# A four-layer graph network with experts: incidence blocks built in steps inside the attention's tile loop

## The chip, the cores and the metric

The kernel is one program on one core of one Trainium2 chip. The metric is the device time of a whole execution in microseconds (us); of several executions the median is taken. Besides, one execution is recorded by the hardware profiler, and all views of the profile are of that one execution. Engines are named as in the profile: PE is TensorE (PEld its weight loads), DVE is VectorE, ACT is ScalarE, POOL is GpSimd, SP is SyncE. [...]in this kernel the order within each queue is fixed when the program is built.

## The reference, cut to what matters

The network has 3125 nodes with 256 features each, and 53125 edges sorted by destination (25000 random edges, the same edges turned round, and one loop per node). Four layers of a graph operation and a mixture of experts follow each other:

```python
x = x + attention(layernorm(x), edge_attr_8, ..., src, dst)   # layer 0, graph
x = x + experts0(layernorm(x), ...)                           # layer 0, experts
x = x + conv1(layernorm(x), ..., edge_index)                  # three hidden convolutions
x = x + experts1(layernorm(x), ...)
x = x + conv2(layernorm(x), edge_index, ...)
x = x + experts2(layernorm(x), ...)
x = x + conv3(layernorm(x), ..., src, dst)
x = x + slices(layernorm(x), ...)
```

Only layer 0 and the preparation of the convolutions matter here:

```python
def attention(nfeat, attn_bias, Wq, Wk, Wv, Wo, src, dst):
    q, k, v = (heads of nfeat @ Wq.T / SCALING, nfeat @ Wk.T, nfeat @ Wv.T)   # 8 heads of 32
    attn = einsum('ehd,ehd->eh', k[src], q[dst]) + attn_bias
    a = exp(attn - segment_max(attn, dst)[dst])
    a = a / segment_sum(a, dst)[dst]
    return segment_sum(v[src] * a, dst) @ Wo.T

def conv(h, ...):            # in each convolution, with weights of its own
    agg = segment_sum(h[src], dst)      # scaled by degrees of destinations or sources
```

The convolutions need sums over edges, `segment_sum(h[src], dst)`. The kernel computes them as dense matrix products: a 3125 x 3125 matrix of counts, whose entry for a pair of nodes is the number of edges between them, times h. That matrix of counts, in two layouts, is what this document calls **the blocks**.

## The kernel before, in words

**Attention.** `attention()` first prepares: `edges_in()` gathers the edges' sources, destinations and biases in windows of 128 edges per partition row and turns them with TensorE, so that an edge lies on a partition (`src_i`, `row_h`, `eb`); beside it layer norm and the projections q, k, v of all nodes are computed, and k and v are stored in DRAM as one table `kv_d` with a row of 512 values per node. Then follows a loop over T = 25 tiles of P = 125 destination nodes. The edges of one tile fill up to WC = 18 chunks of 128 edges, worked in three parts of PC = 6 chunks. For a tile the functions are called in this order, two tiles being under way at a time:

- `one_hot` (L1551): DVE compares, for all edges of the tile, their destination row with 0..124; the result `oh` has 128 x 2250 elements. `one_hot_turned`: PE turns it, ACT copies the result.
- `logits`, once per part: GpSimd issues six gathers (L1574), each of 128 rows of `kv_d` by the index of the source, into a part of a `kv` buffer (seven of them in rotation); PE brings q to the edges (L1582 into `qx`), DVE multiplies k by it (L1585) and sums per head.
- `sums_of` (L1601 with the bias `eb`, an exponential on ACT, 18 small matmuls into `sm`): sums over the edges of a node; `weights_of`: the weights (L1611, L1613).
- `weighted`: DVE multiplies v by the weights (L1621), ACT makes a float copy `oh_f` of the one-hot matrix, PE sums the weighted v in `acc` (L1628). With its last matmul the `kv` buffers are free for gathers of a later tile.
- `normed`, `normed_turned`, `projected`: division by the sums, the product with Wo, and the addition to x.

The scheduler that builds the program may move instructions of the loop against one another on an engine within the limits of the buffers.

**Blocks and first experts.** After the attention `blocks()` and `experts0()` run interleaved: `blocks` is a generator, and `experts0` advances it at nine points in each of its seven groups of three or four tiles. `blocks` divides the nodes of a tile into GT = 25 groups of GN = 5 destinations, G = 625 groups in all, of at most 128 edges each (otherwise a flag sends the run to a general path). From the degrees, which the attention has counted in `deg`, it computes the first edge of each group, stores these 625 numbers in DRAM, gathers the edges of each group by them (L1750), and derives for every edge the row and tile of its source and its column in the group. Then for each of 25 tiles: `hot` compares (L1790: `hr`, `hc` of 128 x 3125 elements, `hs` of 128 x 625), PE counts, with one matmul per group into a "bk" bank of 125 columns (L1802), and degrees of sources into `bdeg` (L1804), seven evacuations take the counts to `ab`, alternately on DVE and ACT (`evacuate`, L173 and L175), `ab` is written to `at_d` in DRAM (L1808), PE turns `ab` piece by piece (L1814), four evacuations take it to `an`, which is written to `an_d` (L1818). Three rows of scales (`to_row`, L1693 to L1699) are written to `rows_d`.

`experts0` loads its weights in `wslot`, and for each group of tiles computes layer norm, gates, hidden layers and the sum, which is added to x (L776); the gates' chain (softmax, choice of two, turning) is short instructions in a row.

The convolutions that follow read `at_d` and `an_d` back.

Of the kernel before, what the change touches and what calls it, by code (L numbers as in the profile page):

```python
# [56 lines left out]
def gnn_ffn_kernel(ctx: ExitStack, tc: tile.TileContext, a, out: bass.AP):  # L57
# [1353 lines left out]
    def attention():  # L1411
# [5 lines left out]
        q_d = dram.tile([P, T, 3, D], BF16, name="q_d")  # L1417
        win_d = dram.tile([T * WC], I32, name="win_d")
        KO, VO, AO = 16, 16 + D, 7
        WB = T * WC // 5  # L1420
        with ExitStack() as es:
            big = es.enter_context(tc.tile_pool(name="att", bufs=1))
            wqkv = big.tile([128, 2, 3 * D], F32, name="wqkv")
# [3 lines left out]
            eb = big.tile([128, H, T * WC], F32, name="eb")  # L1427
# [4 lines left out]


            setup = ExitStack()
            pool = setup.enter_context(tc.tile_pool(name="att_in", bufs=2))
            psum = setup.enter_context(tc.tile_pool(name="ps_in", bufs=2, space=PSUM))
# [50 lines left out]
            def turned(to, b, w):  # L1487
                ps = psum.tile([128, 512], F32, name="tr")
                nc.tensor.transpose(ps[:, :WB], w, ident[:WB, :WB])
                evacuate(to[:, b * WB:(b + 1) * WB], ps[:, :WB])  # L1490

            def edges_in():
# [5 lines left out]
                for name, to in (("src", src_f), ("dst", dst_f)):  # L1498
                    for b, w in windows(a[name].rearrange("(e o) -> e o", o=1), 1, "w_" + name):
                        wf = pool.tile([WB, 128], F32, name="wf")  # L1500
                        nc.vector.tensor_copy(wf, w)
                        turned(to, b, wf)
# [3 lines left out]
                yield  # L1506
                for b, w in windows(a["edge_attr_8"], H, "w_eb"):
                    for h in range(H):
                        turned(eb[:, h, :], b, w.rearrange("p (e h) -> p e h", h=H)[:, :, h])
                    yield  # L1510
# [4 lines left out]
            for i, (t0, n) in enumerate(GROUPS):  # L1515
# [6 lines left out]
                for i_ in range(n):  # L1522
                    p1 = psum.tile([P, 512], F32, name="p1")
                    p2 = psum.tile([P, D], F32, name="p2")
# [17 lines left out]
            psum = es.enter_context(tc.tile_pool(name="ps_att", bufs=3, space=PSUM))  # L1542
# [4 lines left out]
            def one_hot(t):  # L1547
# [7 lines left out]
                nc.sync.dma_start(s.q, q_d[:, t])  # L1555
                return s
# [11 lines left out]
            def logits(s, p):  # L1568

                kv = pool.tile([128, PC, 2 * D + KO], F32, name="kv", bufs=7)  # L1570
# [19 lines left out]
            def sums_of(s):  # L1590
                c = slice(s.t * WC, (s.t + 1) * WC)

                nc.vector.scalar_tensor_tensor(s.l, s.l, 640.0, eb[:, :, c].rearrange("p h c -> p c h"),
# [24 lines left out]
            def weighted(s):  # L1618
                s.acc = psum.tile([P, 512], F32, name="acc", bufs=2)
# [33 lines left out]

            now, before = one_hot(0), None
            one_hot_turned(now)
            for t in range(T + 1):
                if now:
                    logits(now, 0)
                if before:
                    weights_of(before)  # L1660
                    weighted(before)
                after = one_hot(t + 1) if t + 1 < T else None
                if before:
                    normed(before)
                if after:
                    one_hot_turned(after)
                if now:
                    logits(now, 1)
                if before:
                    normed_turned(before)  # L1670
                if now:
                    logits(now, 2)
                if before:
                    projected(before)
                if now:
                    sums_of(now)
                before, now = now, after

# [12 lines left out]
            nc.vector.tensor_reduce(flags[:, 3:4], fan(ok), AX.X, ALU.add)  # L1691

# [8 lines left out]
    def blocks(pool, psum):  # L1701

        ptr_d = dram.tile([G], I32, name="ptr_d")
        iota_h = pool.tile([128, P], BF16, name="iota_h", bufs=1)
        nc.vector.tensor_copy(iota_h, iota[:, :P])

        upto = pool.tile([P, GT], F32, name="upto", bufs=1)
        within = pool.tile([P, GT], F32, name="within", bufs=1)
        gn = pool.tile([P, GT + 1], F32, name="gn", bufs=1)
        nc.vector.tensor_scalar(gn, iota[:P, :GT + 1], float(GN), None, ALU.mult)  # L1710
        nc.vector.tensor_scalar(upto, gn[:, :GT], pcol[:P], None, ALU.is_gt)
        nc.vector.tensor_scalar(within, gn[:, 1:], pcol[:P], None, ALU.is_gt)
        nc.vector.tensor_sub(within, within, upto)
        ps = psum.tile([128, 512], F32, name="bk")
        for i, l in enumerate((upto, ones[:P, :GT], within)):
            nc.tensor.matmul(ps[:GT, i * 128:i * 128 + T], l, deg, start=True, stop=True)
        got = pool.tile([GT, 3, T], F32, name="got", bufs=1)
        nc.vector.tensor_copy(got, ps[:GT, :384].rearrange("p (a t) -> p a t", a=3)[:, :, :T])
        first = pool.tile([GT, T], F32, name="first", bufs=1)
        nil = pool.tile([GT, T], F32, name="nil", bufs=1)  # L1720
        nc.vector.memset(nil, 0.0)
        nc.vector.tensor_tensor_scan(first, got[:, 1, :], nil, 0.0, ALU.add, ALU.add)
        nc.vector.tensor_sub(first, first, got[:, 1, :])
        nc.vector.tensor_add(first, first, got[:, 0, :])
        ptr = pool.tile([GT, T], I32, name="ptr", bufs=1)
        nc.vector.tensor_scalar(ptr, first, float(E - 128), None, ALU.min)
        nc.sync.dma_start(ptr_d.rearrange("(t g) -> g t", g=GT), ptr)

        over = pool.tile([GT, T], F32, name="over", bufs=1)
        nc.vector.tensor_scalar(over, got[:, 2, :], 128.5, None, ALU.is_gt)  # L1730
# [399 lines left out]
```

## Time and profile before

| | |
|---|---|
| timed executions | 4295.15, 4304.97, 4306.31 us; median 4304.97 |
| profiled execution | 4563.24 us; its span 4561.5 us; mean granted clock of TensorE 0.867 |
| busy in the span | PE 83%, PEld 55%, DVE 37%, ACT 19%, POOL 14% |
| preparation of the attention, 0 to 239 us | PE 125.44, DVE 104.34, ACT 41.05, POOL 59.27 us busy; clock 0.78 |
| tile loop of the attention, 239 to 1118 us | shown in the prediction |
| blocks beside the first experts, 1118 to 1671 us | shown in the prediction |
| everything after, 1671 to 4561 us | PE 2672.24, DVE 709.09, ACT 527.92, POOL 120.86 us busy; clock 0.95 |

The page of the profile has the busy time of each engine, the granted clock in 40 slices, the DMA queues, the chain of work that ended last, and the costliest groups of instructions. A group is a line of the code with an engine and an operation: its busy time, the mean duration of one instruction in nanoseconds, and the idle time of its engine just before these instructions, with what released the engine most often. Busy time by stage is a view of its own, as are the waits of a stretch, the timeline of an engine and the chain in order of time. A share over the whole span mixes stages with different limits; the stages are therefore read one by one.

The ends of the experts' seven groups (the last addition at L776 of each) are at 1233.7, 1366.7, 1476.2, 1562.5, 1607.1, 1640.6 and 1671.3 us; the last addition of the attention is at 1118.3 us.

### The profile page before, as it was taken

Reading aid. Unit: us, or ns where it says so; the run is one execution under the profiler, and the core shown is the slowest. Engines: PE = TensorE matmul, PEld = TensorE weight load, DVE = VectorE, ACT = ScalarE, POOL = GpSimd, SP = SyncE. Lnnn points to the kernel's source line nnn. Section 1 sums busy time; section 2 is a strip of 40 time slices with the busy share of each in tenths; the row PEclk is TensorE's granted clock in tenths of the full one; section 3 lists DMA queues with packets and bytes.
Section 4 is the critical chain, followed back from the end, with each engine's and each line's share of the span. In section 5 each row is a group of like instructions: output and inputs, shape, how many; then the busy total and the mean of one; then the engine's idle time right before and its main releaser. Section 6 shows DMA issues by size and latency. Waiting matters only on the chain.

```text
span 4561.5 us, 47103 instructions
## 1 busy us (share of the span) xinstructions
PE 3807.8 (83%) x19103; PEld 2519.1 (55%) x19103; DVE 1675.1 (37%) x3696; ACT 848.6 (19%) x1496; POOL 623.3 (14%) x585
## 2 busy tenths in 40 slices
PE   5466666666688889999999799991998999999996
PEld 3255555555566454555656578881455555554564
DVE  5255555556887550111124611113314111140271
ACT  1111111112223230101101122220202332320030
POOL 1345555452100000000001300005000000000000
PEclk9677777777676689999999899996997999999997
DMA  3444444443232613222222155552320000012100
GB/s 111 151 124 132 132 131 130 130 131 88 77 119 104 235 71 103 75 92 73 83 73 77 51 177 183 185 182 75 106 71 15 14 7 14 12 53 95 54 1 29
DMA packets 283806, 429.65 MB, mean 94 GB/s; under 512 B 32565, under 2 KB 231817, under 8 KB 283578
## 3 DMA queue, kind: packets, MB, share of 16 engines
q1 hardware_dynamic: 189524, 248.19, 16.4%
q0 software_dynamic: 50480, 133.87, 10.2%
q10 hardware_dynamic: 43573, 44.48, 3.0%
q8 instruction: 152, 2.49, 0.2%
q14 instruction: 77, 0.62, 0.0%
HBM read 330.75 MB, written 95.61 MB: 93 GB/s over the span
## 4 chain that ended last, share of the span: by engine, by line
PE 60%; DMA 2%; DVE 2%; ACT 1%; issue 1%; POOL 0%; ACTq 0%; SPq 0%; DVEq 0%; POOLq 0%
PE agg L1865 22%; PE po L207 17%; PE hid_ps L207 12%; PE tr L207 2%; PE row L207 1%; DMA y<-ys_d,row 1%; PE tok L1324 1%; PE po L205 1%; PE tr L197 1%; PE tr L1946 1%; DMA blk<-at_d 0%; POOL y L1079 0%; ACT h L1171 0%; PE s L207 0%; PE tr L1059 0%
## 5 line engine op out<-in xcount | busy, mean ns | idle before, releaser
L1865 PE MATMUL agg<-blk,hp 125*128 125x500 bf16 (+1 forms) x5250 | 1015.0, 354 | 104.2 <-DMA blk<-at_d 97.6
L1865 PEld LDWEIGHTS <-hp 125*128 125x128 bf16 x5250 | 509.7, 97 | 591.7 <-ACT hp L1836 90.7
L1574 POOL DMA_INDIRECT kv<-kv_d,src_w x450 | 472.6, 1050 | 482.1 <-PE acc L1628 285.7
L1887 DVE TENSOR_TENSOR at<-agg,scale_row 128x500 f32<-128x500 f32 (+1 forms) x70 | 41.9, 623 | 858.6 <-PE agg L1865 684.8
L1582 PE MATMUL qx<-q_t,oht 125*128 125x256 bf16 x1350 | 255.7, 366 | 62.1 <-issue 26.6
L1177 DVE SCALAR_TENSOR_TENSOR x<-po,gall,x 125x256 f32<-125x256 f32 x200 | 94.0, 484 | 426.1 <-PE po L207 426.1
L947 POOL DMA_INDIRECT xs_d<-r_l,pos x50 | 59.6, 1193 | 1391.2 <-ACT r_lt L175 1245.6
L207 PE MATMUL hid_ps<-xe,wslot 128*128 128x256 f32 x1024 | 242.3, 389 | 7.7 <-DVE xe L1061 7.3
L1582 PEld LDWEIGHTS <-oht 125*128 125x128 bf16 x1350 | 169.9, 129 | 124.3 <-issue 47.9
L1171 ACT ACTIVATE h<-hid_ps,shift,scale 128x500 f32<-128x500 f32 (+1 forms) x224 | 161.7, 723 | 375.6 <-PE hid_ps L207 366.7
L1628 PE MATMUL acc<-kv,oh_f 128*125 128x265 f32 x900 | 226.8, 415 | 3.4 <-DVE kv L1621 3.4
L207 PE MATMUL po<-wslot,hid 128*128 128x256 f32 x1024 | 226.2, 379 | 0.0
L207 PEld LDWEIGHTS hid_ps<-xe,wslot 128*128 128x128 f32 x1024 | 182.0, 191 | 52.2 <-DVE xe L1061 16.5
L207 PEld LDWEIGHTS po<-wslot,hid 128*128 128x128 f32 x1024 | 194.6, 190 | 26.5
L1628 PEld LDWEIGHTS acc<-kv,oh_f 128*125 128x125 f32 x900 | 183.6, 207 | 42.7 <-DVE kv L1621 4.0
L207 PE MATMUL po<-wslot,h 128*125 128x256 f32 x800 | 203.8, 389 | 0.1
L207 PE MATMUL hid_ps<-h,wslot 128*128 128x500 f32 (+1 forms) x448 | 192.8, 551 | 4.1 <-ACT h L1171 0.5
L1585 DVE TENSOR_TENSOR kv<-kv,qx 128x512 f32<-128x512 f32 x225 | 151.0, 681 | 110.5 <-remote 63.4
L207 PE MATMUL hid_ps<-xt,wslot 128*128 128x500 f32 (+1 forms) x448 | 189.0, 545 | 0.0
L207 PEld LDWEIGHTS po<-wslot,h 128*125 128x125 f32 x800 | 146.6, 189 | 73.0 <-ACT h L1171 25.3
L1068 ACT ACTIVATE hid<-hid_ps,wslot 128x256 f32<-128x256 f32 x256 | 118.5, 474 | 342.7 <-PE hid_ps L207 342.7
L1611 PE MATMUL sm<-m,oht 125*128 125x8 bf16 x450 | 15.6, 168 | 187.7 <-DVE kv L1577 186.6
(449 smaller groups left out, 4839.0 us busy)
## 6 DMA issues: line engine op xcount, KB each, us to landing
wslot<-in_ex_W SPq DMA_DIRECT2D x64, 1024.0 KB
blk<-an_d SPq DMA_DIRECT2D x60, 610.4 KB
xs_d<-nothing ACTq DMA_DIRECT2D x8, 3328.0 KB
blk<-at_d SPq DMA_DIRECT2D x40, 610.4 KB
blk<-an_d SPq DMA_DIRECT2D x45, 457.8 KB
at_d<-ab SPq DMA_DIRECT2D x25, 762.9 KB
an_d<-an SPq DMA_DIRECT2D x25, 762.9 KB
blk<-at_d SPq DMA_DIRECT2D x30, 457.8 KB
```

What stands on the lines that cost most here:

```text
L197: nc.tensor.transpose(ps[:, i * P:(i + 1) * P], src[:, i, k * 128:(k + 1) * 128], ident[:P, :P])
L205: nc.tensor.matmul(ps, ones_h[:, :ps.shape[0]], bias, start=True, stop=False)
L207: nc.tensor.matmul(ps, l, r, start=(bias is None and i == 0), stop=(i == last))
L947: st = nc.gpsimd.indirect_dma_start(out=xs_d, in_=l2[:, i, :], in_offset=None, out_offset=bass.IndirectOffsetOnAxis(ap=self.pos[s][:, t0 + ...
L1068: nc.scalar.activation(hid[:, m, :], ps[:, :BLK], AF.Gelu, bias=c[:, 4 + m:5 + m])
L1171: nc.scalar.activation(dst[:, m, :c], ps[:, :c], AF.Relu, bias=shift[:, l, col:col + 1], scale=scale[:, l, col:col + 1])
L1177: nc.vector.scalar_tensor_tensor(x[:, t0 + i, :], po, gall[:, t0 + i, e:e + 1], x[:, t0 + i, :], ALU.mult, ALU.add)
L1574: nc.gpsimd.indirect_dma_start(out=kv[:, c, KO:], out_offset=None, in_=kv_d, in_offset=bass.IndirectOffsetOnAxis(ap=src_i[:, at:at + 1], a ...
L1582: nc.tensor.matmul(ps[:, c, :], s.oht[:, p * PC + c0 + c, :], s.q[:, k, :], start=(k == 0), stop=(k == 2))
L1585: nc.vector.tensor_mul(k_, k_, ps)
L1628: nc.tensor.matmul(s.acc[:, :D + H + 1], of[:, c, :], kv[:, c, AO:VO], start=(p == 0 and c == 0), stop=(p == 2 and c == PC - 1))
L1865: nc.tensor.matmul(to[f], l, parts[m // MB][:, :, m % MB, :], start=(m == 0 and k == 0), stop=(m == T - 1 and k == 2 and not own))
```

## The change

`blocks()` is replaced by a class `Blocks`, whose work is cut into steps and called from the attention:

- `begins()`, in the preparation of the attention, counts the first edge of each group directly from `row_h` (a comparison with 26 bounds in two halves, then 18 matmuls with one row of output for each half), instead of from the degrees after the attention, and takes the 625 numbers through DRAM.
- `steps()` is a generator, advanced six times in each pass of the tile loop; what is left is done after the loop. Window gathers and window arithmetic are done for five tiles at a time (`fetch`, `turn_windows`), the comparisons in three parts per tile (8, 8 and 9 groups), one part ahead of the counts. All evacuations of the blocks are on ACT. `an_d` is written in four pieces per tile.
- `ends_in()`, after the loop, writes the three rows of scales and the flag.
- `experts0()` then runs alone.
- Room for it: the bias `eb` goes to DRAM (`eb_d`) in the preparation and is read back per tile; the projection weights `wqkv` move to the pool of the preparation; `kv` has eight buffers instead of seven; the attention's PSUM pools shrink (`qx` and `sm` from three banks to two, `acc` from two to one, `p2` to one).

Numbers of lines in the diff are those of the kernel before; comparisons, counts and turns keep their shapes but for the three parts.

```diff
@@ attention(), preparation @@
+        eb_d = dram.tile([128, T, H, WC], F32, name="eb_d")
...
-            wqkv = big.tile([128, 2, 3 * D], F32, name="wqkv")
-            eb = big.tile([128, H, T * WC], F32, name="eb")
+            built = Blocks(es.enter_context(tc.tile_pool(name="blocks", bufs=2)),
+                           es.enter_context(tc.tile_pool(name="ps_blocks", bufs=2, space=PSUM)))
...
+            wqkv = pool.tile([128, 2, 3 * D], F32, name="wqkv", bufs=1)
...
+                yield from built.begins(pool, psum, row_h, first[:, :T])
                 for b, w in windows(a["edge_attr_8"], H, "w_eb"):
+                    eb = pool.tile([128, 5, H, WC], F32, name="eb")
                     for h in range(H):
-                        turned(eb[:, h, :], b, w.rearrange("p (e h) -> p e h", h=H)[:, :, h])
+                        turned(eb[:, :, h, :], w.rearrange("p (e h) -> p e h", h=H)[:, :, h])
+                    nc.sync.dma_start(eb_d[:, b * 5:b * 5 + 5], eb)
...
-                    p2 = psum.tile([P, D], F32, name="p2")
+                    p2 = psum.tile([P, D], F32, name="p2", bufs=1)
@@ attention(), tile loop @@
-            psum = es.enter_context(tc.tile_pool(name="ps_att", bufs=3, space=PSUM))
+            psum = es.enter_context(tc.tile_pool(name="ps_att", bufs=2, space=PSUM))
...
+                s.eb = pool.tile([128, H, WC], F32, name="eb_t")
+                nc.sync.dma_start(s.eb, eb_d[:, t])
...
-                kv = pool.tile([128, PC, 2 * D + KO], F32, name="kv", bufs=7)
+                kv = pool.tile([128, PC, 2 * D + KO], F32, name="kv", bufs=8)
...
-                s.acc = psum.tile([P, 512], F32, name="acc", bufs=2)
+                s.acc = psum.tile([P, 512], F32, name="acc", bufs=1)
...
+            steps = built.steps()
             for t in range(T + 1):
                 if now:
                     logits(now, 0)
+                next(steps, None)
...
                 if now:
                     sums_of(now)
                 before, now = now, after
+            for _ in steps:
+                pass
...
+            built.ends_in()
@@ blocks() -> class Blocks @@
+        def begins(self, pool, psum, row_h, first):
...
+            for g0 in (0, half):
+                below = pool.tile([128, half, T, WC], BF16, name="b_below", bufs=1)
+                nc.vector.tensor_tensor(
+                    below.rearrange("p g t c -> p g (t c)"),
+                    row_h.unsqueeze(1).to_broadcast([128, half, T * WC]),
+                    edge[:, g0:g0 + half].unsqueeze(2).to_broadcast([128, half, T * WC]), ALU.is_lt)
+                ps = psum.tile([128, 512], F32, name="tr")
+                for c in range(WC):
+                    nc.tensor.matmul(ps[:1, :half * T], one, below[:, :, :, c],
+                                     start=(c == 0), stop=(c == WC - 1))
...
+        def steps(self):
+            PARTS = ((0, 8), (8, 8), (16, 9))
...
+            def count(t, j, hot, ab):
...
-                evacuate(ab[:, :, g0:g0 + n, :],
-                         ps[:P, :n * P].rearrange("p (g s d) -> p s g d", g=n, d=GN))
+                    nc.scalar.copy(ab[:, :, first + g0:first + g0 + m, :],
+                                   ps[:P, :m * P].rearrange("p (g s d) -> p s g d", g=m, d=GN))
...
+                an = pool.tile([P, 8 * P], BF16, name="an")
+                nc.scalar.copy(an[:, :n * P].rearrange("p (s r) -> p s r", s=n),
+                               ps.rearrange("p (s r) -> p s r", s=8)[:P, :n, :P])
+                nc.sync.dma_start(an_d[:, t, s0 * P:(s0 + n) * P], an[:, :n * P])
...
+            for t in range(T):
+                ab = pool.tile([P, T, GT, GN], BF16, name="ab")
+                if t % 5 == 2 and t + 3 < T:
+                    got = self.fetch((t + 3) // 5)
+                for j in range(3):
+                    if j < 2:
+                        after = hots(t, j + 1)
+                    elif t + 1 < T:
+                        if t % 5 == 4:
+                            yield from self.turn_windows((t + 1) // 5, got)
+                        after = hots(t + 1, 0)
+                    count(t, j, hot, ab)
+                    hot = after
+                    yield
+                    if old is not None:
+                        turn(t - 1, 8 * j, old)
+                        if j == 2:
+                            turn(t - 1, 24, old)
+                        yield
+                nc.sync.dma_start(at_d[:, t, :], ab.rearrange("p s g d -> p (s g d)"))
+                old = ab
...
@@ weights("main") @@
-                steps = blocks(bp, bps)
-                experts0(steps)
-                for _ in steps:
-                    pass
+        experts0()
```

## The prediction, written before the result was known

> **What bounds the kernel now.** I read the page first, then busy time by stage, then the waits and the timeline of one attention tile, then the chain of waits. The page's first line gives the span; its costliest groups show GpSimd with half its time in waits for the weighted sums:
>
> ```profile
> span 4561.5 us, 47103 instructions
> ...
> L1574 POOL DMA_INDIRECT kv<-kv_d,src_w x450 | 472.6, 1050 | 482.1 <-PE acc L1628 285.7
> ```
>
> Busy time by stage (start:end, length, then PE, PEld, DVE, ACT, POOL busy with instruction counts, granted clock, DMA share, GB/s): the tiles of the attention; the start of the blocks; the 25 blocks with the first three groups of the experts; the experts' other four groups.
>
> ```profile
> 239.00:1118.00 879.00, 580.00 (x3576) 458.43 (x3576) 483.30 (x701) 141.75 (x263) 430.10 (x408) 0.73 0.44 127
> 1118.00:1182.00 64.00, 34.58 (x109) 17.45 (x108) 44.91 (x165) 13.88 (x22) 13.04 (x11) 0.70 0.28 67
> 1182.00:1533.00 351.00, 283.47 (x2150) 224.13 (x2150) 287.29 (x351) 101.88 (x160) 0.00 (x0) 0.67 0.28 109
> 1533.00:1671.00 138.00, 112.12 (x320) 56.52 (x318) 46.21 (x177) 22.11 (x37) 0.00 (x0) 0.77 0.58 207
> ```
>
> In the blocks TensorE and VectorE are busy 81% and 82%: that stage is full. In the attention VectorE is busy 55%. Five tiles alone, then the waits of the stage (engine, line, released by: total, times, longest):
>
> ```profile
> 507.60:695.30 187.70, 122.03 (x751) 96.44 (x750) 100.96 (x145) 29.77 (x55) 95.37 (x91) 0.72 0.46 131
> ```
> ```profile
> POOL kv L1574 <- PE acc L1628: 285.7, 21, 23.7
> DVE sums L1601 <- remote: 251.3, 22, 13.0
> ```
>
> One tile takes 187.7/5 = 37.5 us: TensorE 24.4 us, VectorE 20.2. GpSimd issues for 24.5 us and stands for 13, until a kv buffer is free.
>
> **How much of that idle time is real.** The profiled execution took 4563.24 us, 1.7 beyond its span; the median of the timed runs is 4304.97, 258 less. No work in the trace can shrink by that much, but one kind of wait can: L1601 waits 251.3 us for nothing the trace names ("remote"), only in this stage, though the matmuls it needs had started 10 us earlier. I take it that these waits belong to the profiled execution. About 30 us of such waits lie before 239 us, on L1585; the other 228, over 22 tiles, are 10.4 each. So a tile of the timed runs takes about 27 us, with GpSimd (24.5 us of issuing, more when VectorE blocks it) as its bound and little idle left. This is the disputed point; a rival below takes the other side.
>
> **What the Trainium skill says.** "SBUF — State Buffer", Who interferes with whom: a VectorE instruction with two SBUF inputs contends with a GpSimd instruction that reads SBUF; the later one blocks. (The page also infers that tensor_tensor leaves descriptor generation alone; the trace decides.) The trace agrees with the contention:
>
> ```profile
> 657.10 0.95 POOL L1574 DMA_INDIRECT kv<-kv_d,src_w  x1 [13.24 <-PE acc L1628]
> 658.36 2.74 POOL L1574 DMA_INDIRECT kv<-kv_d,src_w  x1 [0.30 <-issue]
> ```
> ```profile
> 657.77 2.50 DVE L1551 TENSOR_TENSOR oh<-iota_a,row_w 128x2250 bf16<-128x2250 bf16 x1
> ```
>
> The gather beside the 2.50 us comparison took 2.74 instead of 0.95: 1.8 us lost. "TensorE: Matmul & The Clock Gate", What's actually happening: the default clock is half speed and recent activity releases it. The trace agrees: 0.73 granted in the attention, 0.67 in the blocks.
>
> **The change, part by part.**
>
> Removed, the separate stage. From the last x of the attention (1118) to the last of the experts (1671) it takes 553 us. What remains is the experts alone. The chain has the ends of their last groups:
>
> ```profile
> 1607.14 0.42 DVE x L776
> 1640.62 0.43 DVE x L776
> 1671.27 0.56 issue
> ```
>
> A group of three tiles takes 33.5 and 30.7 us, say 32; one of four, with 4/3 of the matmuls but the same gate chain of 6 us, about 40. 4x40 + 3x32 = 256, plus 12 until the first weights are there and 8.6 (ACT's issue at L225 in the chain): about 277. **Saved: 276**, bounds 255 and 300. The chain's 10.7 us wait for a rows_d write at 1533 goes with it.
>
> Added to the tiles. The built order of instructions shows what the scheduler did: 58 of the 625 counts stand before the first sums matmul, 42 after the last; between, one block of 25 per tile with few exceptions. Per block, from its own rows:
> - VectorE: the comparisons at L1790 took 187.1 us in 75 pieces, 7.5 per block; the same elements in nine pieces. The window arithmetic of five blocks at once (20 instructions of 0.2 to 0.3) adds 1. Evacuations go to ACT. 20.2 + 7.5 + 1 = 28.7.
> - TensorE: (77.3 + 60.5 + 67.2)/25 = 8.2 for counts, degrees and transposes. 24.4 + 8.2 = 32.6 at the clock of the trace.
> - ACT: seven evacuations of 0.59 and three of 0.99 and small ones, 7.6, on 6.0: no bound, but in TensorE's path, because there are two "bk" banks.
> - GpSimd: two index gathers in five tiles, 0.5; and the comparisons have two SBUF inputs, so they block gathers. At L1551's rate (1.8 of 2.5) 7.5 us cost 5.4; window arithmetic 0.3. 27 + 6.2 = 33.2. Bounds: nothing for the short pieces (27.5), or all (35.3).
> The largest is GpSimd at 33.2, TensorE 0.6 below; for queues in order that wait for each other I add 1.2: 34.4, or +7.4 on 27. Over 22 tiles **+163**, bounds +75 (TensorE warmer, half the blocking) and +330 (rival below).
>
> Added ahead of the tiles: begins() compares 2 x 5850 elements at 1.09 ns (L1790: 3406 ns for 3125), 12.8 us of VectorE; 36 one-row matmuls of 325 columns, no row for that form, 5 to 10 us if scaled by columns from the 125-column counts (0.06 to 0.13 issue to issue); copies and a pointer round trip through DRAM, some 5 us; five eb_d writes; and 2.3 blocks. Before 239 us VectorE is busy 104 of 239 us and TensorE 125, so most is covered; but kv gathers start only when that pool is closed. **+20**, bounds 0 and +45.
>
> Added after the tiles: about 1.7 blocks, 14 us each alone (351/25), behind the last tile's 18 us: +15. And the first weights of the experts now wait for the three rows_d writes: the chain saw one take 10.7 us: +12. **+27**, bounds +10 and +50.
>
> At nothing: kv buffers 7 to 8 (GpSimd is already a tile ahead in the timed case; a gain of 1 us per tile is the lower bound); eb read per tile from DRAM, 25 loads on SP, and an_d in four writes, all a tile ahead on SP, whose queue is otherwise empty here (if one is late, the sums wait for the 2 us of a load); acc, qx, sm and p2 with fewer banks: VectorE empties them in 0.4 to 0.7 us, and the buffers' owners are a tile apart. DMA: 1.56 MB per tile on 4.9, some 190 GB/s in 34 us, where gathers alone run at 210.
>
> **Sum.** -276 + 163 + 20 + 27 = -66, rounded to -70 for the one us per tile that kv's eighth buffer may give in part: 4305 - 70 = **4235 us**. Against the profiled execution: there the tile has 13 us of standing GpSimd and 13 of TensorE to take the block, and I expect 40 us a tile, +55: 4563 - 276 + 55 + 47 = 4389. That the profile gains more than the timed runs is part of the forecast.
>
> **Rivals.**
> 1. *The idle time is real* (the timed runs gain their 258 us elsewhere). For it: a wait is a wait, and the blocks need only 8 us of the 13. Against: it has no releaser, and the stages at full clock have nothing to give. Then tiles grow by 1, the blocking that the standing time can't take: -276 + 22 + 20 + 27 = -207, 4098.
> 2. *Slower: TensorE stands for evacuations.* A block has 11 round trips TensorE-ACT-TensorE over two "bk" banks (in the blocks stage TensorE waited 35 us for ab evacuations, 17 for an, with two engines to do them). Now ACT does all, behind oh_f casts that wait 5 us for acc. If each trip costs 0.7 us, it is 7.7 on TensorE, in front of the attention's own matmuls; acc is late, so kv buffers and gathers are: 42 us a tile, +15, +330: -276 + 330 + 47 = +101, 4406. It decides from a tile of (276 - 47)/22 = 10.4 above 27: 37.4 us. Against: the scheduler places other matmuls between a count and the next.
> 3. *It doesn't spread*: the blocks pile up at one end and the stage only moves. The built order speaks against it; about 4300.
>
> **Chances.** Main 0.55, with a range of its own from 4150 to 4310; rival 1 0.25; rival 2 0.18; rival 3 0.02. Under 0.3% (13 us) a measurement of this kernel can hardly tell from none. Main gives faster in nine of ten, so faster 0.5 + 0.25 = 0.75, same 0.05, slower 0.20. The range 4080 to 4390 takes in rival 1 and the lower part of rival 2.
>
> **What would show it.** In the profile after: no stage of blocks between the attention and the experts, and those take about 277 us; GpSimd's gathers longer on the mean than 1050 ns, by about 0.3 us; the attention's tiles near 40 us in the profiled execution; one pool of standing GpSimd time, smaller than 285.7. Wrong would be: tiles over 45 us there, with TensorE waiting on ACT at the evacuations (rival 2); a gather beside a comparison of 1.1 us that is no longer than 0.95; the timed runs gaining as much as the profiled one (rival 1).

## The result, and the profile after

The changed kernel takes 4353.72 us (median of four executions, 4346.08 to 4356.25) where the kernel before takes 4300.06 (4288.13 to 4306.31): a ratio of 1.0125, interval 1.0097 to 1.0153. It is slower, by some 54 us; 4235 was forecast. The profiled execution, 4352.25 us, is one of the four.

One thing must be known to read any number here: chips differ. On some, each of these kernels takes 200 to 340 us longer, and where a version has a profile from both kinds, nearly all of it lies in the attention's tile loop. By its time and its waits, the profile of before on record comes from such a chip (4563); its timed executions come from others (4300). So every experiment is set against the kernel before on the same chip, and "on a 4300 chip" or "on a 4590 chip" says what the kernel before took there. No chip was used at two times, so what is called the chip here may be something else that stayed the same meanwhile.

The page of the profile after, its first line and the gathers (busy, mean ns | idle before, releaser):

```profile
span 4350.1 us, 47519 instructions
...
L1582 POOL DMA_INDIRECT kv<-kv_d,src_w x450 | 527.1, 1171 | 335.6 <-PE acc L1635 172.8
```

GpSimd stands 172.8 us for the weighted sums and a gather takes 1171 ns on the mean. The 285.7 us and 1050 ns of the profile of before are from the other kind of chip and can't be set against these; a pair from one chip follows with the controls. Busy time by stage (start:end, length, then PE, PEld, DVE, ACT, POOL, clock, DMA share, GB/s): tile loop, end of the blocks, first experts, a stage that no step of the prediction has, and all the rest:

```profile
265.00:1105.90 840.90, 657.72 (x5193) 553.58 (x5191) 654.64 (x978) 276.08 (x503) 478.08 (x407) 0.82 0.56 175
1105.90:1141.00 35.10, 9.31 (x75) 7.21 (x73) 20.01 (x90) 9.99 (x19) 0.00 (x0) 0.55 0.36 110
1141.00:1395.70 254.70, 212.98 (x672) 105.69 (x672) 82.04 (x288) 35.12 (x62) 0.00 (x0) 0.87 0.03 9
1395.70:1454.00 58.30, 0.25 (x2) 0.01 (x1) 7.30 (x32) 0.00 (x0) 0.00 (x0) 0.51 1.06 376
1454.00:4350.00 2896.00, 2682.85 (x12473) 1692.99 (x12473) 710.75 (x2051) 530.03 (x928) 120.65 (x100) 0.94 0.24 77
```

From 1395.7 to 1454.0 TensorE does next to nothing and the DMA engines are full (1.06, 376 GB/s). The chain of waits has the reason:

```profile
1395.05 0.43 DVE x L776
1395.48 0.28 DVE nothing L222
...
1402.14 8.84 ACTq L225
...
1411.02 8.38 ACTq L225
...
1445.31 8.73 ACTq L225
1454.07 1.28 ACT L186
```

L225 is `clear_slots`, called at the head of the first convolution: eight transfers from a small tile of zeros, `nothing`, fill the 27.3 MB of `xs_d`, and ScalarE stands while they are issued; the layer norm (L186) is behind them in its queue. In the kernel before the same eight were issued earlier, beside the experts' groups (shortest, median and longest issue in ns, then first and last start); in the changed kernel they stand behind them:

```profile
L225 ACTq DMA_DIRECT2D xs_d<-nothing x8: 681/7162/9214, 1545.2 to 1597.3; - x8
```
```profile
L225 ACTq DMA_DIRECT2D xs_d<-nothing x8: 677/8556/8840, 1395.9 to 1445.3; - x8
```

`nothing` is set (L222) right after the experts' last addition: that is what one would see if it lay where the experts' buffers lie. An experiment below tries this.

The waits of the tile loop (window 245 to 1105; engine, line, released by: total, times, longest) have a second newcomer, and the timeline of ScalarE shows it in one tile:

```profile
ACT oh_f L1633 <- PE acc L1635: 175.8, 58, 7.3
ACT an L1851 <- DMA an_d<-an: 168.0, 19, 14.0
ACT ab L1841 <- PE bk L1836: 109.3, 67, 6.3
```
```profile
603.46 0.59 ACT L1841 CAST ab<-bk 125x500 bf16<-125x500 f32 x1
618.03 0.99 ACT L1851 COPY an<-bk 125x1000 bf16<-125x1000 bf16 x1 [13.99 <-DMA an_d<-an]
618.92 0.60 ACT L1841 CAST ab<-bk 125x500 bf16<-125x500 f32 x1
```

ScalarE stands 14 us until an `an` buffer has been written to DRAM. There are two of them, each for a third of a tile, so a buffer is wanted again two pieces later; behind the waiting copy stand the exponentials and the float one-hot copies, without which acc and the next gathers don't start. Why the write is so late, SyncE's queue shows:

```profile
597.56 0.25 SPq L1878 DMA_DIRECT2D at_d<-ab  x1
597.90 0.29 SPq L1561 DMA_DIRECT2D q_t<-q_d  x1
600.44 1.83 SPq L1853 DMA_DIRECT2D an_d<-an  x2
```

The pieces of `an` were issued behind the write of a whole tile of `ab` (763 KB) and a load of q. The trace's DMA packets of this queue, told apart by their sizes (6250, 1536 and 2000 bytes), run in that order: at_d's from 599.3 to 607.8 us, q's from 607.3 to 612.2, those of the first piece from 609.2 to 617.2. Each of the 17 waits over 5 us ends 11 to 21 us after an at_d write was issued.

### The profile page after: what moved, and what is told of

The parts are those of the page before. It is cut to its first block, busy times and chain, and to the rows that moved or that the text cites. A ratio compares the mean times of both kernels' runs of the same rounds, so it can differ in the third digit from the quotient of the medians.

```text
span 4350.1 us, 47519 instructions
## 1 busy us (share of the span) xinstructions
PE 3736.9 (86%) x19133; PEld 2463.3 (57%) x19133; DVE 1632.3 (38%) x3783; ACT 909.0 (21%) x1628; POOL 677.8 (16%) x585
## 4 chain that ended last, share of the span: by engine, by line
PE 67%; DMA 4%; DVE 3%; ACTq 1%; ACT 1%; issue 1%; POOL 0%; SPq 0%; DVEq 0%; POOLq 0%
PE agg L1937 23%; PE po L207 19%; PE hid_ps L207 13%; PE tr L207 3%; DMA y<-ys_d,row 1%; ACTq L225 1%; PE row L207 1%; PE po L205 1%; PE tok L1324 1%; DMA an_d<-an 1%; PE tr L197 1%; PE acc L1635 1%; PE pair L207 1%; PE tr L2018 0%; ACT h L1171 0%
## 5 line engine op out<-in xcount | busy, mean ns | idle before, releaser
L1582 POOL DMA_INDIRECT kv<-kv_d,src_w x450 | 527.1, 1171 | 335.6 <-PE acc L1635 172.8
L1635 PE MATMUL acc<-kv,oh_f 128*125 128x265 f32 x900 | 251.1, 445 | 26.1 <-ACT oh_f L1633 13.2
L1590 PE MATMUL qx<-q_t,oht 125*128 125x256 bf16 x1350 | 220.3, 312 | 35.0 <-DVE kv L1593 29.5
L1635 PEld LDWEIGHTS acc<-kv,oh_f 128*125 128x125 f32 x900 | 195.4, 221 | 77.7 <-DVE kv L1628 18.1
L207 PEld LDWEIGHTS po<-wslot,hid 128*128 128x128 f32 x1024 | 194.6, 190 | 26.5
L1590 PEld LDWEIGHTS <-oht 125*128 125x128 bf16 x1350 | 143.2, 112 | 70.0 <-issue 40.3
L1836 PE MATMUL bk<-hc,hr 128*125 128x125 bf16 x625 | 83.9, 264 | 110.3 <-ACT an L1851 69.8
L207 PE MATMUL po<-wslot,lt 128*125 128x256 f32 x600 | 159.6, 395 | 2.3 <-DVE lt L173 1.3
## 6 DMA issues: line engine op xcount, KB each, us to landing
xs_d<-nothing ACTq DMA_DIRECT2D x8, 3328.0 KB
```

The costliest lines, as they stand in the source:

```text
L207: nc.tensor.matmul(ps, l, r, start=(bias is None and i == 0), stop=(i == last))
L1582: nc.gpsimd.indirect_dma_start(out=kv[:, c, KO:], out_offset=None, in_=kv_d, in_offset=bass.IndirectOffsetOnAxis(ap=src_i[:, at:at + 1], a ...
L1590: nc.tensor.matmul(ps[:, c, :], s.oht[:, p * PC + c0 + c, :], s.q[:, k, :], start=(k == 0), stop=(k == 2))
L1635: nc.tensor.matmul(s.acc[:, :D + H + 1], of[:, c, :], kv[:, c, AO:VO], start=(p == 0 and c == 0), stop=(p == 2 and c == PC - 1))
L1836: nc.tensor.matmul(ps[:P, (g - g0) * P:(g - g0 + 1) * P], hr[:, g, :], hc[:, g, :], start=True, stop=True)
```

## Experiments

**Controls: which chip, which profile.** The changed kernel and the kernel before, unaltered, and the kernel before cut after the attention.

> The kernel before, cut after the attention: x as the attention leaves it is written out, and blocks, experts, convolutions and slices are left out. Theory A (the 258 us by which the profiled execution exceeds the timed ones are the waits 'remote' of the attention's tile loop): the profiled execution takes about 1130 us, the timed ones about 870. Rival B (the timed executions gain their 258 us in other stages): both take about 1130.

Measured, on a 4590 chip: two executions, 1148.23 us (the profiled one) and 1152.68. The execution without the profiler is no shorter, so the "remote" waits (257.6 us at L1601) are not the profiler's: rival B's numbers, though its reason, a gain in other stages, is nothing that this run could show.

> The changed kernel unaltered, as the control of the other runs, with a profile of its own. The first experiments ran where the kernel before takes 4590 us, not 4300, so they can't be set against the changed kernel's 4354. Theory A: where the kernel before takes 4590, the changed one takes about 4590 to 4600 (the clearing's pause of 58 us on top of the 4536 of the version without it); where the kernel before takes 4300, 4350. Rival B: the edit of the experts' address did nothing: then the changed kernel takes 4536 where the one before takes 4590.

> The kernel before unaltered, for its profile on the same chip as the changed one. Theory A: the profiled execution takes as long as the timed ones on the same chip, within 0.5%; if the chip gives 4300, the 251 us of remote waits before the sums are gone from the trace and a tile of the attention takes 25 to 27 us; if it gives 4590, they are there. Rival B (the profiler makes these waits): they are in the trace in either case, and the profiled execution is 250 us longer than the timed ones.

Measured, where the kernel before takes 4548: changed kernel 4564.09, ratio 1.0039 (1.0025 to 1.0053); kernel before profiled at 4542.86, with its remote waits (229.5 us). From the kernel before to the changed one on this chip, GpSimd's waits for the weighted sums grow from 245.2 to 361.9 us, the mean gather from 1046 to 1117 ns, and a tile from 35.8 to 42.7 us (22 tiles, from the first x addition). Stages of the changed kernel there, tile loop and the rest:

```profile
265.00:1306.00 1041.00, 702.97 (x5360) 586.48 (x5360) 681.25 (x1011) 286.12 (x515) 456.05 (x404) 0.76 0.47 142
...
1653.00:4553.00 2900.00, 2682.38 (x12473) 1691.07 (x12473) 711.56 (x2051) 529.78 (x928) 120.77 (x100) 0.94 0.25 77
```

The same program takes 1041 us in the loop where the other chip took 841, and the same time elsewhere within 4 us. 

> The kernel before unaltered, for a profile where it takes about 4300 us. Theory A: the remote waits before the sums are gone, the attention ends near 850 us, its tile takes 25 us with VectorE busy 80% of it and TensorE's clock near 0.9, and the stages after it are as long as in the profile on record. Rival B: the 258 us are missing in other stages.

This fell on a 4590 chip as well (4590.11), so its theory stays open: the kernel before has no profile from a 4300 chip, and its tile there is inferred below. None of the profiles from 4300 chips, of other versions, has a remote wait in the tile loop.

**An unused buffer below the experts.**

```diff
-        experts0()
+        with tc.tile_pool(name="pad", bufs=1) as pp:
+            pad = pp.tile([128, 79680 // 4], F32, name="pad")
+            nc.vector.memset(pad[:, 0:1], 0.0)
+            experts0()
```

> The changed kernel with an unused buffer of 79,680 bytes held below the first experts' pool while they run, so that this pool lies where it lay in the kernel before and no longer over the small zero tile from which xs_d is cleared. Nothing is left out. Theory A (the clearing of xs_d, eight transfers of 8.6 us that stand alone between 1396 and 1454 us in the changed kernel, has moved behind the experts because its source tile shares addresses with them): the clears run beside the experts' groups, the pause goes, the experts get 10 to 25 us longer because ScalarE stands for the transfers, and the time falls by 35 to 55 us, to about 4305. Rival B (the 27 MB of clearing need the memory's bandwidth wherever they stand, and the first convolution waits for them all the same): under 10 us, 4345.

> The version with an unused buffer below the first experts' pool, so that the source of the clearing shares no address with it; nothing left out. Theory A: 35 to 60 us under the changed kernel on the same chip. Rival B (bandwidth): within 10 us of it.

> The unused buffer below the first experts' pool alone. Theory A (the pause is in a stage without gathers, so its price is the same on every chip): 45 to 55 us under the changed kernel's 4354, about 4304. Rival B (where the tile loop is faster something else takes its place): under 30 us.

Measured: 4536.64 on a 4590 chip (0.9892 of the kernel before, 0.9870 to 0.9914); 4514.17 beside the changed kernel's 4564.09, 50 us less; 4309.27 on a 4300 chip, 1.0021 (1.0008 to 1.0034) against 1.0125, some 45 us less. In that last run the clears start at 1128 instead of 1396 us:

```profile
L225 ACTq DMA_DIRECT2D xs_d<-nothing x8: 542/825/4470, 1128.2 to 1202.6; - x8
```

But for one small memset only addresses were moved, so it is the shared address that held the clears back. Of the pause's 58 us, 45 to 50 come back: with the clears among them, the stages from the attention's last addition to the experts' last take 305 us (1102.8 to 1408.2) instead of 290 (1105.5 to 1395.0). There ScalarE is held 11.4 us by the eight issues and stands 17.8 and 14.0 us for two loads of weights beside them; which of the two costs the 15 us was not settled.

**Eight `an` buffers** (and seven kv buffers, for room; the two were not tried apart).

```diff
-                an = pool.tile([P, 8 * P], BF16, name="an")
+                an = pool.tile([P, 8 * P], BF16, name="an", bufs=8)
-                kv = pool.tile([128, PC, 2 * D + KO], F32, name="kv", bufs=8)
+                kv = pool.tile([128, PC, 2 * D + KO], F32, name="kv", bufs=7)
```

> The changed kernel with eight buffers for the turned pieces 'an' instead of two, and seven kv buffers instead of eight to make room. Nothing is left out. Theory A (ScalarE stands 168 us for writes of an_d, up to 14 us in each tile, because a piece's buffer is free only when its write has landed, and everything behind it on ScalarE, the evacuations of counts and the float one-hot copies, is late): that wait falls under 20 us, tiles go from 34.9 to 31 us or less, the time falls by 70 to 110 us, to about 4265. Rival B (ScalarE's wait only fills idle time; the tile is set by TensorE with GpSimd slowed by comparisons): waits move to the acc and bk matmuls, tiles stay over 34 us, under 20 us gained, 4340.

> Eight an buffers and seven kv buffers, nothing else, nothing left out; wanted where the kernel before takes 4300 us. Theory A (the tile stands for the writes of an_d; with plain loads eight buffers were worth 74 us): with the gathers in place 50 to 90 us under the changed kernel's 4354, about 4285. Rival B (with the gathers in place GpSimd, slowed by the comparisons, bounds the tile and the wait fills its time): under 20 us, 4340.

Measured: on a 4590 chip 4572.32, 0.9966 (0.9950 to 0.9981) of the kernel before; the changed kernel wasn't run on that chip. On a 4300 chip 4239.82, 0.9846 (0.9818 to 0.9875) against 1.0125 for the changed kernel: 2.8%, some 115 to 120 us. ScalarE's waits there no longer name an_d (window 245 to 1000):

```profile
ACT oh_f L1633 <- PE acc L1635: 189.7, 73, 7.3
ACT ab L1841 <- PE bk L1836: 119.2, 71, 6.4
ACT an L1851 <- PE bk L1848: 101.9, 65, 6.0
```

Attention tiles take 30.2 us ((992.9 - 268.8)/24, from the x additions) instead of 34.9. Theory A, and more than it asked. The writes are as late as before: in the same place of this trace the packets of an_d come from 610.8 to 623.2 us, behind at_d's. The additional buffers hide that; whether another queue for at_d would do as well was not tried.

**Both.**

> Both edits together: the unused buffer below the first experts, and eight an buffers with seven kv buffers. Theory A: the two gains add, since they lie in different stages: 105 to 165 us, about 4220, which is under the kernel before (4300). Rival B: neither wait bounds its stage; about 4340.

> That buffer, eight an buffers and seven kv buffers; nothing left out. Theory A: where the kernel before takes 4300, the an wait of 168 us bounds the tile, and this takes 60 to 110 us less than the version with the unused buffer alone; where the kernel before takes 4590, other waits bound the tile and the two are within 10 us. Rival B: no difference in either case, as TensorE and the gathers set the tile.

> Both edits. Theory A: 100 to 145 us under the changed kernel's 4354, about 4230, which is 1.6% under the kernel before where that takes 4300. Rival B: the gains don't add, over 4270.

Measured: 4194.81 on a 4300 chip, 0.9742 (0.9714 to 0.9770) of the kernel before: 1.0125 - 0.9742 = 3.8% under the changed kernel, and 1.0 + 2.8 for the two alone. They add, and this version beats both kernels. On 4590 and 4548 chips 4534.85 and 4510.77, no more than 4 us under the version with the unused buffer alone: there the an buffers bring nothing. That the remote waits set the loop on those chips is likely, but not shown.

> Both edits, and the eight clears of xs_d issued by SyncE instead of ScalarE. Nothing is left out. Theory A (beside the experts ScalarE still stands 15 to 30 us for the clears it issues, in front of the experts' activations): 10 to 25 us under the version with both edits, about 4178 where that takes 4195. Rival B (the clears' bandwidth delays the experts' weights and the blocks' first loads in either case, or SyncE's queue holds these behind the clears): no gain or a loss up to 20.

Measured, on another 4590 chip: 4525.37, 0.9855 (0.9827 to 0.9884), against 0.9889 (0.9861 to 0.9916) for both edits on the first. The intervals overlap: not settled.

**What bounds the tile: plain loads for gathers.**

```diff
-                for c in range(PC):
-                    at = s.t * WC + p * PC + c
-                    nc.gpsimd.indirect_dma_start(...)
+                r0 = (s.t * 3 + p) * 31
+                nc.gpsimd.dma_start(kv[:, :, KO:], kv_d[r0:r0 + PC * 128, :].rearrange("(c e) d -> e c d", c=PC))
```

> The kernel before with the six gathers of a part of the attention replaced by one plain load of 768 consecutive rows of kv_d, issued by GpSimd: as many bytes, other nodes' k and v. Theory A (the remote waits, 230 to 258 us before the sums where the kernel takes 4550 to 4590, are made by the gathers' many descriptors): the remote waits go, TensorE (24.4 us a tile) sets the tile, 22 to 26 us instead of 35 to 37, the attention ends near 850. Rival B (they come from elsewhere, a lower clock or the memory): tiles stay over 33 us.

> The changed kernel with the same replacement of gathers by one plain load per part: other nodes' k and v. Theory A (in the changed kernel a tile is set by TensorE's order and by ScalarE standing for the writes of an_d, not by the gathers): tiles take 30 to 34 us, hardly less than the 34.9 of its profile on record, and ScalarE waits over 150 us for an_d. Rival B (the comparisons block the gathers, and GpSimd sets the tile): 28 us or less, TensorE's own busy time.

> The version with plain loads, of the changed kernel, with eight an buffers and seven kv buffers. Theory A (ScalarE's wait for an_d sets part of the tile where no gather disturbs): the wait is gone, and the tile is 2 us or more shorter than with two an buffers, near TensorE's and VectorE's busy times of 29 us. Rival B (the wait fills idle time): within 1 us of the version with two an buffers.

Measured, one execution each, all on one 4300 chip (4296.99): 4162.11, 4296.12 and 4222.49 us. As such a chip shows no remote waits with gathers either, plain_before's question, what makes them, stays open. In this kernel before, a tile takes 20.8 us; twelve of them:

```profile
350.00:600.00 250.00, 224.84 (x1795) 183.75 (x1793) 237.51 (x347) 68.78 (x132) 29.70 (x36) 1.00 0.66 236
```

VectorE is busy 95% of the time and sets the tile. TensorE, whose 24.4 us a tile were to be the bound, needs 224.84/12 = 18.7 us at a clock of 1.00 instead of 0.72. Where changed tiles have no gathers they take 32.4 us ((1043.5 - 265.6)/24), and 30.2 with eight an buffers: rival B of plain_after is out, and the an wait costs 74 us here. The 30.2 us are also what tiles take with eight an buffers and all their gathers, so it isn't the gathers that set them. Ten of those tiles without gathers, VectorE busy 90%:

```profile
450.00:750.00 300.00, 250.82 (x2124) 213.35 (x2123) 268.85 (x411) 110.92 (x200) 25.79 (x30) 0.87 0.59 209
```

**Steps after the loop.** All six `next(steps, None)` of the loop are taken out.

> The changed kernel with the six calls that advance the blocks inside the tile loop taken out, so that all steps are issued after the loop; the scheduler still moves some five blocks up between the first tiles, and the tiles from the fourteenth to the twenty-first hold next to none. Nothing is left out. Theory A (the block work is what lengthens a tile, and fewer PSUM banks, the eighth kv buffer and the bias from DRAM cost nothing): those tiles take what tiles of the kernel before take on the same chip, within 1 us. Rival B (the smaller PSUM pools hold the attention up): they take 2 us or more longer. The blocks alone, some 19 after the loop, then take 10 to 14 us each.

Measured, one execution on the same chip: 4434.94 us. The tiles with next to no block work, then the blocks alone:

```profile
600.00:800.00 200.00, 168.78 (x1208) 132.44 (x1208) 164.81 (x253) 48.84 (x91) 157.86 (x139) 0.88 0.67 195
895.00:1215.00 320.00, 167.79 (x1388) 158.97 (x1386) 171.28 (x314) 126.95 (x211) 0.00 (x0) 0.51 0.28 97
```

Those tiles, the fourteenth to the twenty-first, take 25.4 us (from the x additions), with a clock of 0.88. The kernel before, on this chip, ends its attention near 4297 - 2 - (4159.9 - 706.6) = 842 us if the rest is as long as in plain_before. Less 39 us for the last two tiles and 256 for the first, both as on slower chips, 22 tiles take 24.9 us each; but 35 of the 256 are remote waits, and if all of these fall away it is 26.5. So a tile of the kernel before takes 25 to 26.5 us by inference, and the smaller PSUM pools cost little, if anything. The 19 blocks take 320/19 = 17 us each, not 10 to 14; ScalarE stands for writes of an_d for 130 of the 320 us here too.

**Comparisons made once.** `hots` keeps what it makes for the first tile, with six an and seven kv buffers.

> The changed kernel with six an and seven kv buffers, and the block comparisons made for the first tile only and used for all (VectorE loses 7.2 us of work a tile; the blocks are those of the first tile, so every later layer has other numbers). Theory A (with the an wait gone VectorE bounds the tile at 29 us, and its comparisons are 7.5 of them): tiles near 25 to 27 us where the kernel before takes 4300, mean gather back at 1050 ns. Rival B (TensorE with ScalarE's evacuations bounds the tile): under 1.5 us less than with the comparisons.

Measured, on a 4300 chip: 4137.26, 0.9608 (0.9580 to 0.9636), against 0.9846 with eight an buffers and all comparisons: 2.4%, some 100 us, 4 us a tile. The same 300 us with all comparisons (eight an buffers) and with these:

```profile
450.00:750.00 300.00, 253.08 (x2096) 214.88 (x2095) 267.86 (x405) 113.45 (x204) 213.08 (x176) 0.87 0.67 208
```
```profile
450.00:750.00 300.00, 257.70 (x2178) 217.94 (x2177) 245.08 (x377) 126.30 (x232) 236.51 (x206) 0.95 0.75 239
```

With all comparisons VectorE is busy 89%, GpSimd 71%; without them a tile gets from 30 to 26 us. The gathers on 4300 chips, with all comparisons and eight an buffers, with those of the first tile alone, and with the steps after the loop:

```profile
L1582 POOL DMA_INDIRECT kv<-kv_d,src_w x450 | 540.8, 1202 | 222.1 <-issue 116.4
```
```profile
L1582 POOL DMA_INDIRECT kv<-kv_d,src_w x450 | 510.3, 1134 | 162.3 <-issue 114.0
```
```profile
L1582 POOL DMA_INDIRECT kv<-kv_d,src_w x450 | 520.1, 1156 | 162.4 <-issue 117.3
```

Gathers take 1134 ns on the mean without the comparisons, not 1050 as expected. Perhaps other instructions of VectorE hinder them too where less time is idle; that was not tried. On such chips the comparisons thus add 1202 - 1134 = 68 ns to a gather.

## Why the prediction was wrong, point by point

The forecast's sum beside what was measured on 4300 chips, in us (attention: to its last addition, against the 842 inferred above; stage: from there to the end of the first experts, pause included, against 563 in plain_before; rest: against 2890 there):

| | forecast | changed kernel | with both edits |
|---|---|---|---|
| attention, with what is ahead of it (+163 and +20) | +183 | +264 | +140 |
| separate stage (-276 and +27) | -249 | -215 | -253 |
| rest | 0 | +6 | +6 |
| sum | -66 | +55 | -107 |

**"Saved: 276": one of eight clears was counted.** "What remains is the experts alone" was false. The experts took 254.7 us for 256 forecast, but the eight clears of xs_d came to stand after them. The chain of before showed one of the eight (8.64 us at L225), the list of DMA issues had all: "xs_d<-nothing ACTq DMA_DIRECT2D x8, 3328.0 KB". The sum took one for the stage's start. What was missed is a move that the diff doesn't show: without the pool of the blocks below it, the experts' pool slid down over the addresses of `nothing`. Price, shown: 45 to 50 us.

**"At nothing: ... an_d in four writes, all a tile ahead on SP": the step that turned the sign.** The queue was not "otherwise empty": at_d's 763 KB go through it once per tile, and in the tile shown a piece of an_d issued behind them came to its end 17 us later. And the buffers no longer cover that: two of a whole tile became two of a third, so ScalarE's queue stands up to 14 us behind a write. Price, shown with seven kv buffers: 115 to 120 us on a 4300 chip. It is this that turned the sign: with the wait and without the pause the ratio is 1.0021, with the pause and without the wait 0.9846. With both out of the way the kernel takes 4195 (both_third), where 4235 was forecast: the rest of the sum was some 40 us too dear.

**"I take it that these waits belong to the profiled execution": wrong,** by before_att. They go with the chip. The tile of the timed executions was nevertheless nearly right, 25 to 26.5 us by inference for 27. The forecast for the profile, 4563 to 4389 with the block's work taken up by the 13 us of standing time (+2.5 us a tile), can be set against the 4548 chip, which has these waits in both kernels: there a tile grew by 6.9 us and the time by 16 instead of falling by 174.

**The tile, 34.4 us forecast, 34.9 measured:** right in the number by luck, not in its parts. VectorE, forecast at 28.7 us, is the nearest bound: with the an wait gone a tile takes 30.2 us, with or without gathers, and VectorE is busy 27.1 of them. Taking 6.5 us of its work took 4 us from the tile, so something else is close behind; TensorE is then the busiest, 87% of the loop. GpSimd's 33.2 was too much. That a comparison blocks a gather is seen again, timeline of GpSimd and of VectorE:

```profile
605.85 1.26 POOL L1582 DMA_INDIRECT kv<-kv_d,src_w  x1 [0.30 <-issue]
607.41 1.59 POOL L1582 DMA_INDIRECT kv<-kv_d,src_w  x1 [0.30 <-issue]
609.31 0.95 POOL L1582 DMA_INDIRECT kv<-kv_d,src_w  x1 [0.30 <-issue]
```
```profile
605.10 1.19 DVE L1823 TENSOR_TENSOR hr<-iota_h,b_row_h 128x1000 bf16<-128x1000 bf16 x1
...
606.99 1.19 DVE L1823 TENSOR_TENSOR hc<-iota_h,b_col_h 128x1000 bf16<-128x1000 bf16 x1
```

but by the 68 ns above all comparisons together cost a tile's 18 gathers 18 x 0.07 = 1.2 us, where 5.4 were taken from one 2.5 us comparison. The an wait filled what was over. Two smaller terms: the base was 25 to 26.5, not 27, and the last two tiles, 39 us together before, took 62 and were not counted.

**Ahead and behind: inside the bounds.** The first gather shows what came ahead, before and after:

```profile
L1574 POOL DMA_INDIRECT kv<-kv_d,src_w x450: 943/949/2784, 166.7 to 1079.2; - x150
```
```profile
L1582 POOL DMA_INDIRECT kv<-kv_d,src_w x450: 942/949/3277, 199.3 to 1040.6; - x150
```

It starts 33 us later (+20 forecast, bounds 0 and +45); on the 4548 chip the starts are 167.0 and 201.4, so this doesn't hang on the chip. The end of the blocks took 35 us (+27 forecast).

**Rivals.** Rival 1 is out: tiles grew by 6.9 us even where the chip has the idle time, not by 1. Rival 2 had the sign and the engine, ScalarE in the path of a tile, but not the mechanism: with the write's wait gone, two "bk" banks and all evacuations on ScalarE are there still, and tiles fall to 30 us. Rival 3 is out: 35 us of blocks are left behind the loop, where steps_last, with 19 blocks piled up there, has 320.

## What to carry to other kernels

When work is cut into pieces, count each buffer anew in pieces: how many are there, how long does the write that frees one take, what is issued ahead of that write in its queue, and what stands behind the one that waits. When a pool is moved or removed, look at which later buffers share its addresses: work that ran early because its buffer was free will silently come late. And before a wait in a profile is called the profiler's, compare with a timed execution on the same chip.

## What was not expected of the hardware

The same program takes 4353.72 us on one chip and 4564.09 on another; the 200 us lie in the gather loop, where the slower chips show waits whose releaser the trace doesn't name ("remote": 119.6 us at L1593 and 165.3 at L1851 in the changed kernel, 229.5 to 257.6 at L1601 in the one before). What makes them was not settled.

TensorE's busy time for a tile's attention went from 24.4 us at a clock of 0.72 (the profile of before) to 18.7 at 1.00 (plain_before), and was 21.4 at 0.88 in steps_last, on the same chip as plain_before (168.78/200 of a tile's 25.4 us, a small piece of a block with it). In these three the clock is higher where TensorE is busy for more of the time, 65%, 90% and 84%. Its busy time can't be added up as if it were fixed.

A comparison hindered GpSimd's gathers but not its plain loads. In plain_after a plain load issued 0.3 us after the start of a 2.50 us comparison took 0.83 us, and all 75 took 827 to 894 ns, while gathers beside comparisons took 1.26, 1.59 and 2.74 us instead of 0.95. Why they differ was not tried.
